# A graph layer with residual and layer norm: put and code turns in the unused columns of the pick banks, ranking products at the end of the step before, bias rows behind the table's stores

## The chip, the cores and the metric

One core of a Trainium2 chip runs the kernel. The metric is the device time of one execution in microseconds (us); lower is better. Engines are named as the profile names them: PE is TensorE (PEld its weight loads), DVE is VectorE, ACT is ScalarE, POOL is GpSimd, SP is SyncE, which here only issues DMAs. "L614" is line 614 of the kernel before.

## The reference

The graph has 12,500 nodes with 128 features and 400,000 edges that are sorted by their destination. Each edge has a type, 0 or 1. What is computed, cut to what matters:

```python
Xs = x[src]
m_data = Xs @ W_data.T + b_data
m_ctrl = Xs @ W_control.T + b_control
msg = where(edge_type == 0, m_data, m_ctrl)
agg = segment_sum(msg, dst, num_segments=12500)
h = x + relu(agg + (x @ W_self.T + b_self))
out = (h - mean(h)) / sqrt(var(h) + 1e-5)
```

## The kernel before, in words

**The idea.** Weights are linear, so the kernel first adds up the source rows of each destination node, apart for the two edge types, and counts them; the product with W_data and W_control, the counts times the biases, the self term and the norm come once for each node ("finish"). A float32 row is held as three bf16 parts (384 columns), so that bf16 matmuls add it up without loss.

**Tiling.** The 3125 blocks of 128 edges fall into 25 groups of 125 blocks, and each group into windows of two kinds. "p" windows (5 blocks, 865 blocks in all) gather their source rows from a table in DRAM, rows3, by an indirect DMA on POOL for each block (`msg`, L721), and are added up by a selection matrix `psel` (L671, L747). "e" windows (20 blocks, 113 windows) take their source rows from a copy of the table in SBUF, x3, with matmuls. The main loop has one step for each e window, 113 steps; the p blocks are spread through it.

**An e window w** goes through these stages; each names its function:

- `give_slots(w)` sorts the window's 2560 edges into 100 cells (node blocks) of 32 places each. `block_matrix`, `fours` and `same_lane` (DVE) write a one-hot matrix O and sums of it (`prod`). `before` (PE, L550) multiplies these with triangular matrices, the *ranking products*, into the bank `rk`; L492 adds a column for the spares of the window before it. `ranks` (DVE, L560 to L575) turns them into each edge's place within its cell, and `rank_matrix` into `rv` (L602). `over` (DVE) picks out the few edges that have no place in their cell and counts them (`over_n`).
- `put` (PE, L614, 20 full-width matmuls of 64 columns) writes node numbers and codes into their cells, in columns 0 to 63 of `rk`. `spread` copies them to SBUF (`cell`, ACT, L622), and two DMAs on SP send the node numbers through DRAM to all partitions (`there`, `pick`).
- `turn_codes` (PE, L634, four 128x32 matmuls of 25 columns, into columns 100 to 124 of `rk`) and `keep_codes` (ACT, L644) turn the codes. With them run the third and fourth part of `spare_slots` for window w-1: seven matmuls (L502) with the 128x64 matrices `om`, three ACT and DVE copies, and so the row numbers `idx` of the spares.
- `pick_matrix(w)` (DVE, L656) makes `pick` one-hot.
- `picked(w)` is the step itself, in six *units* t = 0 to 5. Each unit does two pairs of `rows(q)`: eight `pick` matmuls of 128x32 (L769) write two banks of a `got` tile, 384 of the 512 columns in each, and ACT copies both into `emsg` (L780). There are two `got` tiles, used in turn. A unit also does `count(q)` for four q of the unit before it (L798, 128x32) and `add` (L671, twelve full-width matmuls of 176 columns). Unit 2 gathers the spares' rows (`spare_rows`, POOL, L784, into `last`), unit 5 does `last_rows` (two more picks and an ACT copy, L793). `choose` (DVE, L476) makes the selection matrices `esel` for eight or nine q. `end` adds the last q and accumulates the window's sums into `acc` (DVE, L709); it is called as `ending` in unit 0 of the next step.

**The order of the work.** Each step hands lists of (position, function) to `merged`, which calls them by position; unit t stands at (t + 0.5) / 6. In step w, before the change: the ranking products of window w+2 in unit 1, `ranks` at 0.26, `rank_matrix` at 0.3, the spares' `om` at 0.28, `over` at 0.75; O, `fours` and `same_lane` of window w+3 at 0.55; `pick_matrix(w+1)` at 0.6; `put` and `spread` of window w+2 at the end of unit 4; its `turn_codes` and `keep_codes` in `end`. From the calls, the framework builds one queue for each engine, which it may order otherwise where operands are ready at other times; on the chip each queue is worked off in order. `rk` is one bank; the products of window w+3 can only be written when every reader of window w+2's is done.

**Start-up.** `split_x` loads x, splits it into x3 (L254 to L257) and stores it as the table rows3 with eight SP DMAs (L261). Meanwhile `all_slots` puts windows 0 and 1 into their cells. Then come, in the order of the calls: the loads of group 1 (L193 to L201, 21 DMAs), `bparts`, which splits the biases on one partition (DVE) and writes them into nine places of `bias` by 27 SP DMAs (L405, L407), `pick_matrix(0)`, the first slots of window 2, `store_rows`, and 14 `fetch` calls (POOL gathers of p blocks). `bias` is first read by the finishing products (L894).

Of the kernel before, what the change touches and what calls it, by code (L numbers as in the profile page):

```python
# [151 lines left out]
def short_path(ctx, tc, const, ident, eps, wT, brow, bad, x, src, dst, etype, ws, bs, out):  # L152
# [172 lines left out]

    ltri = keep.tile([P, 4, P], BF, name="ltri")
# [67 lines left out]

    def bparts():

        part = tmp.tile([1, 3, 3, D], BF, name="part")
        rest = tmp.tile([1, 3, D], FP, name="rest")
        nc.vector.tensor_copy(part[:, 0], brow)
        nc.vector.tensor_tensor(rest, brow, part[:, 0], op=OP.subtract)  # L400
        nc.vector.tensor_copy(part[:, 1], rest)
        nc.vector.tensor_tensor(part[:, 2], rest, part[:, 1], op=OP.subtract)
        for at in [at + k for at in range(0, P, CAP) for k in (0, 3)]:
            for j in range(3):
                nc.sync.dma_start(out=bias[at + j:at + j + 1, :, :], in_=part[:, j, 0:2, :])  # L405
        for j in range(3):
            nc.sync.dma_start(out=bias[6 + j:7 + j, 0, :], in_=part[:, j, 2, :])  # L407
# [76 lines left out]
    def spare_slots(w, rk):  # L484


        if w < 0:
            return [lambda: None] * 4
        s = slots[w]

        def over_before():
# [4 lines left out]
        def over_matrix():  # L496
            om = s["om"] = two.tile([P, TOP, OVF], BF, name="om", bufs=1)
            nc.vector.tensor_scalar(om, slot_col, rk[:, 500:501], None, op0=OP.is_equal)

        def turn():  # L500
            for k in range(TOP):
                nc.tensor.matmul(  # L502
                    rk[:OVF, 504:507], s["om"][:, k, :], s["bits"][:, :, k],
# [3 lines left out]
        def keep():  # L507
            code = s["code"][:OVF, NQ - 1:NQ]
            nc.scalar.copy(code, rk[:OVF, 506:507].rearrange("p (n o) -> p n o", o=1).to_broadcast(list(code.shape)))
            part = two.tile([OVF, 2], FP, name="part")  # L510
            nc.scalar.copy(part, rk[:OVF, 504:506])
# [6 lines left out]
    def give_slots(w):  # L518
# [26 lines left out]
        def before():  # L545
# [8 lines left out]
            spares = s["spares"] = spare_slots(w - 1, rk)  # L554
            spares[0]()
# [53 lines left out]
        def put():  # L609


            for c in range(EC):
                m = P if c < EC - 1 else NCELL
                nc.tensor.matmul(  # L614
                    s["rk"][:m, :2 * CAP], s["held"][:, c * NCELL:c * NCELL + m], s["rv"][:, c].rearrange("p v r -> p (v r)"),
# [15 lines left out]
        def turn_codes():  # L631

            for a in range(4):
                nc.tensor.matmul(  # L634
                    s["rk"][CAP * a:CAP * (a + 1), 100:100 + NQ], s["cell"][:, CAP:], ident_b[:, a * NQ:(a + 1) * NQ],
                    start=True, stop=True, skip_group_check=True,
                )
            s["spares"][2]()

        def keep_codes():  # L640
            rk = s["rk"]
            code = s["code"] = two.tile([P, NQ, 2], BF, name="code")
            at = rk[:, 100:100 + NQ].rearrange("p (n o) -> p n o", o=1)
            nc.scalar.copy(code, at.to_broadcast(list(code.shape)))  # L644
            s["spares"][3]()
# [107 lines left out]
    def picked(w, tiled, ending, fin_used, before):  # L753
# [20 lines left out]
        def rows(q):  # L774
            ps = psg.tile([P, pair, 512], FP, name="got")
            msg = two.tile([P, pair, 3 * D], BF, name="emsg", bufs=5)
            for k in range(pair):
                pick(ps[:, k, :3 * D], q + k)
                s["msg"][q + k] = msg[:, k, :]
            nc.scalar.copy(msg, ps[:, :, :3 * D])  # L780

        def spare_rows():
            msg = s["msg"][NQ - 1] = two.tile([P, 3 * D], BF, name="last")
            nc.gpsimd.indirect_dma_start(  # L784
                out=msg[:OVF, :], out_offset=None, in_=rows3[:, :],
                in_offset=bass.IndirectOffsetOnAxis(ap=slots[w]["idx"], axis=0),
            )
# [19 lines left out]
        def unit(t):  # L807

            for q in range(t * per, (t + 1) * per, pair):
                rows(q)  # L810
            if t == 1 and before:
                before()
# [367 lines left out]
```

## Time and profile before

| what | value |
|---|---|
| median of three runs | 2107.02 us (2105.46 to 2108.23) |
| the profiled execution | 2095.26 us, of which the span is 2093.6 us |
| busy in the span: PE, DVE, ACT, POOL | 1836.4, 1720.3, 1304.5, 1305.9 us |
| TensorE clock granted, mean | 0.978 |
| picks L769 | 10896 matmuls, 663.5 us busy |
| sums L671 of esel | 8136 matmuls, 761.9 us busy |
| copy emsg L780 | 1356, 803 ns each |
| gathers msg L721 | 865, 1350 ns each |

Busy is the time in which at least one instruction of the engine runs. Matmuls overlap, so the length of one matmul says little, and the distance from start to start is what a stream of them costs. A wait is the idle time of an engine just before an instruction, put down to what came last of all that the instruction needed. The profile is of one execution, and its own time (2095.26 us) is the one to compare its parts with.

### The profile page before, as it was taken

What the parts mean: (1) busy time and instruction counts of PE and PEld (TensorE: products, weight loads), DVE (VectorE), ACT (ScalarE), POOL (GpSimd) and SP (SyncE); (2) the same over time, 40 slices, a digit from 0 to 9 for tenths busy, and PEclk for the clock granted to TensorE, in tenths of its full rate; (3) what the DMA queues carried; (4) which work ended last, traced back from release to release, by engine and by line L of the source; (5) the groups of instructions that cost most, each with busy time, mean ns of one, the idle gap of its engine ahead of it and who ended that gap; (6) DMA issues with size and microseconds to landing.
All of it is one profiled execution on the core that took longest, in us unless ns stands there. A gap on an engine that the chain in (4) does not pass through costs nothing.

```text
span 2093.6 us, 75473 instructions
## 1 busy us (share of the span) xinstructions
PE 1836.4 (88%) x30869; PEld 1376.5 (66%) x30869; DVE 1720.3 (82%) x4707; ACT 1304.5 (62%) x2464; POOL 1305.9 (62%) x996
## 2 busy tenths in 40 slices
PE   0669889999999998999999999999999999999996
PEld 0446667666766676666666666766776676766675
DVE  7958889888888888888888878878888888878873
ACT  4535666666666665666666666656666666656665
POOL 0167667667667566667666556575667667766760
PEclk9989999999999999999999999999999999999998
DMA  7643443443443443433433434434434434434321
GB/s 187 193 123 115 122 136 101 137 135 100 133 135 99 135 133 95 137 111 117 135 108 108 127 99 136 131 100 134 132 102 132 131 111 131 120 105 130 124 96 32
DMA packets 187343, 254.92 MB, mean 122 GB/s; under 512 B 86202, under 2 KB 153804, under 8 KB 183916
## 3 DMA queue, kind: packets, MB, share of 16 engines
q1 hardware_dynamic: 129226, 152.97, 22.7%
q0 software_dynamic: 45136, 90.65, 15.5%
q10 hardware_dynamic: 12626, 6.40, 1.2%
q8 instruction: 243, 3.98, 0.8%
q14 instruction: 112, 0.92, 0.1%
HBM read 231.87 MB, written 18.03 MB: 119 GB/s over the span
## 4 chain that ended last, share of the span: by engine, by line
PE 57%; DVE 28%; issue 5%; ACT 5%; DMA 2%; SPq 1%; POOL 1%; DVEq 0%; another core or an unknown queue 0%; ACTq 0%; POOLq 0%
PE sums L671 25%; PE got L769 19%; ACT emsg L780 4%; DVE esel L476 3%; PE rk L614 3%; DVE pick L656 3%; DVE prod L564 3%; DVE rv L602 2%; PE sums L798 2%; PE fin L894 2%; DVE found L573 2%; DVE prod L542 2%; PE rk L502 2%; DVE ahead L560 2%; PE rk L550 1%
## 5 line engine op out<-in xcount | busy, mean ns | idle before, releaser
L721 POOL DMA_INDIRECT msg<-rows,pidx x865 | 1167.3, 1350 | 697.9 <-PE sums L671 236.2
L780 ACT CAST emsg<-got 128x768 bf16<-128x768 f32 x1356 | 1036.1, 803 | 522.6 <-PE got L769 387.6
L671 PE MATMUL sums<-esel,emsg 128*128 128x176 bf16 x8136 | 761.9, 242 | 14.3 <-issue 13.4
L769 PE MATMUL got<-x,pick 128*32 128x384 bf16 x10896 | 663.5, 334 | 77.5 <-ACT emsg L780 43.8
L671 PEld LDWEIGHTS <-emsg 128*128 128x128 bf16 x8136 | 603.0, 99 | 174.6 <-issue 157.6
L769 PEld LDWEIGHTS <-pick 128*32 128x32 bf16 x11074 | 258.7, 95 | 232.6 <-issue 131.2
L476 DVE TENSOR_TENSOR esel<-code_col,code 128x1408 bf16<-128x1408 bf16 x339 | 308.6, 910 | 31.7 <-PE sums L671 14.1
L709 DVE TENSOR_TENSOR acc<-acc,sums 128x352 f32 (+2 forms) x238 | 102.0, 428 | 175.3 <-PE sums L671 85.8
L671 PE MATMUL sums<-psel,msg 128*128 128x48 bf16 x2595 | 187.3, 185 | 17.5 <-issue 7.2
L798 PE MATMUL sums<-esel,one_col 128*32 128x176 bf16 x2825 | 181.7, 244 | 7.0 <-issue 6.3
L784 POOL DMA_INDIRECT last<-rows,idx x113 | 134.4, 1189 | 56.4 <-issue 16.5
L671 PEld LDWEIGHTS <-msg 128*128 128x128 bf16 x2595 | 150.7, 98 | 26.0 <-issue 23.6
L614 PE MATMUL rk<-rv,O 128*128 128x64 bf16 x2260 | 90.8, 195 | 70.9 <-DVE rv L602 64.8
L656 DVE TENSOR_SCALAR pick<-pick,lane_f 128x1600 bf16<-128x1600 bf16 x226 | 143.2, 639 | 8.5 <-issue 5.0
L614 PEld LDWEIGHTS <-O 128*128 128x128 bf16 x2260 | 83.1, 100 | 99.2 <-issue 98.3
L747 PE MATMUL sums<-psel,one_col 128*128 128x48 bf16 x865 | 145.9, 183 | 0.5 <-issue 0.5
L476 DVE TENSOR_TENSOR O<-cell_col,blk 128x2000 bf16<-128x2000 bf16 x113 | 134.6, 1191 | 12.2 <-PE fin L769 4.7
L564 DVE TENSOR_TENSOR prod<-O,ahead 128x2000 bf16<-128x2000 bf16 x113 | 134.4, 1189 | 0.0
L560 DVE TENSOR_REDUCE ahead<-rk 128x100 bf16<-128x500 f32 x113 | 76.2, 674 | 53.5 <-PE got L769 21.0
L798 PEld LDWEIGHTS <-one_col 128*32 128x32 bf16 x2825 | 86.6, 96 | 47.5 <-issue 17.7
L747 PEld LDWEIGHTS <-one_col 128*128 128x128 bf16 x865 | 82.9, 96 | 1.0 <-issue 0.9
L573 DVE TENSOR_REDUCE found<-half 128x20 f32<-128x520 bf16 x113 | 77.1, 683 | 0.0
(173 smaller groups left out, 2030.2 us busy)
## 6 DMA issues: line engine op xcount, KB each, us to landing
pick<-there SPq DMA_DIRECT2D x113, 800.0 KB
acc<-acc_start SPq DMA_DIRECT2D x23, 1280.0 KB
msg<-rows,pidx POOLq DMA_INDIRECT x865
rows<-x SPq DMA_DIRECT2D x6, 1344.0 KB
xs<-in_x_dram SPq DMA_DIRECT2D x99, 62.5 KB
out_dram<-h SPq DMA_DIRECT2D x99, 62.5 KB
xt<-in_x_dram ACTq DMA_DIRECT2D x6, 896.0 KB
there<-cell SPq DMA_DIRECT2D x113, 6.2 KB
```

The source lines that it names most:

```text
L476: nc.vector.tensor_tensor(sel.rearrange("p n (w t) -> p n w t", t=2), col[:rows].rearrange("p (o w t) -> p o w t", o=1, t=2).to_broadcast( ...
L564: nc.vector.tensor_tensor(prod, s["O"], ahead.rearrange("p (o j) -> p o j", o=1).to_broadcast([P, EC, NCELL]), op=OP.mult)
L573: nc.vector.tensor_reduce(found, half[:, :, :26], AX.X, OP.add)
L614: nc.tensor.matmul(s["rk"][:m, :2 * CAP], s["held"][:, c * NCELL:c * NCELL + m], s["rv"][:, c].rearrange("p v r -> p (v r)"), start=(c == ...
L656: nc.vector.tensor_scalar(t, t, lane_f, None, op0=OP.is_equal)
L671: nc.tensor.matmul(out, msg[:, j * D:(j + 1) * D], sel, start=(start and j == 0), stop=stop, skip_group_check=True)
L721: nc.gpsimd.indirect_dma_start(out=msg[:, k, :], out_offset=None, in_=rows3[:, :], in_offset=bass.IndirectOffsetOnAxis(ap=codes["p", g][0] ...
L747: nc.tensor.matmul(cnt, one_col, sel, start=False, stop=(c == n - 1), skip_group_check=True)
L769: nc.tensor.matmul(ps[CAP * a:CAP * (a + 1), :], slots[w]["pick"][:, a * NQ + q, :], x3[:, 4 * q + a - a0].rearrange("p j d -> p (j d)"), ...
L780: nc.scalar.copy(msg, ps[:, :, :3 * D])
L784: nc.gpsimd.indirect_dma_start(out=msg[:OVF, :], out_offset=None, in_=rows3[:, :], in_offset=bass.IndirectOffsetOnAxis(ap=slots[w]["idx"], ...
L798: nc.tensor.matmul(cells_of(s["ps"], EW, 1)[CAP * (q % 4):CAP * (q % 4 + 1), :], one_col[:, :CAP], s["sel"][q], start=(q < 4), stop=(q + 4 ...
```

## The change

Put writes columns 384 to 511 of the second `got` bank of unit 5's second pair, and the code turns and the spares' products those of unit 0's second pair in the step after. In unit 5 the counts, the last picks (unless finishing work is in the step) and put come between the pair's picks and its ACT copy. `rk` then serves the ranking products alone; those of window w+3 are issued at the end of unit 5 of step w. `ranks` goes to position 0.02, `rank_matrix` to 0.1, `om` to 0.2. `om` becomes a kept tile with one more block of zeros, and its seven products take 128 columns of weights (two neighbouring blocks), so that they have the full width. In the start-up, the split biases go to DRAM with one DMA; after the table's stores come the spares' gather for step 0, nine DMAs for the bias rows, and the loads of group 1.

The diff, cut to its core:

```diff
+    om_all = keep.tile([P, TOP + 1, OVF], BF, name="om_all")
+    nc.vector.memset(om_all, 0.0)
...
+    b_parts = dram.tile([3, 3, D], BF, name="b_parts")
     def bparts():
...
+        nc.sync.dma_start(
+            out=b_parts.rearrange("j i d -> (j i d)").rearrange("(o e) -> o e", o=1),
+            in_=part.rearrange("o j i d -> o (j i d)"),
+        )
+
+    def bias_rows():
         for at in [at + k for at in range(0, P, CAP) for k in (0, 3)]:
-            for j in range(3):
-                nc.sync.dma_start(out=bias[at + j:at + j + 1, :, :], in_=part[:, j, 0:2, :])
-        for j in range(3):
-            nc.sync.dma_start(out=bias[6 + j:7 + j, 0, :], in_=part[:, j, 2, :])
+            nc.sync.dma_start(out=bias[at:at + 3, :, :], in_=b_parts[:, 0:2, :])
+        nc.sync.dma_start(out=bias[6:9, 0, :], in_=b_parts[:, 2, :])
...
-        def over_matrix():
-            om = s["om"] = two.tile([P, TOP, OVF], BF, name="om", bufs=1)
-            nc.vector.tensor_scalar(om, slot_col, rk[:, 500:501], None, op0=OP.is_equal)
+        def over_matrix(rk):
+            nc.vector.tensor_scalar(om_all[:, :TOP], slot_col, rk[:, 500:501], None, op0=OP.is_equal)
-        def turn():
+        def turn(at):
+            om = om_all.rearrange("p k o -> p (k o)")
             for k in range(TOP):
                 nc.tensor.matmul(
-                    rk[:OVF, 504:507], s["om"][:, k, :], s["bits"][:, :, k],
+                    at, om[:, k * OVF:k * OVF + P], s["bits"][:, :, k],
...
-        def put():
+        def put(at):
...
-                    s["rk"][:m, :2 * CAP], s["held"][:, c * NCELL:c * NCELL + m], ...
+                    at[:m, :2 * CAP], s["held"][:, c * NCELL:c * NCELL + m], ...
-        def spread():
+        def spread(at):
             cell = s["cell"] = two.tile([P, 2 * CAP], BF, name="cell")
-            nc.scalar.copy(cell, s["rk"][:, :2 * CAP])
+            nc.scalar.copy(cell, at[:, :2 * CAP])
...
-                    s["rk"][CAP * a:CAP * (a + 1), 100:100 + NQ], s["cell"][:, CAP:], ...
+                    at[CAP * a:CAP * (a + 1), :NQ], s["cell"][:, CAP:], ...
-            s["spares"][2]()
+            s["spares"][2](at[:, 32:35])
...
-        s["tiled"] = {4: [put, spread], 6: [turn_codes, keep_codes]}
+        s["put"], s["turn"] = (put, spread), (turn_codes, keep_codes)
...
-            (0.1, before), (0.26, ranks), (0.28, lambda: s["spares"][1]()), (0.3, rank_matrix), (0.75, over),
+            (0.02, ranks), (0.2, lambda: s["spares"][1](s["rk"])), (0.1, rank_matrix), (0.75, over),
...
-        def rows(q):
+        def rows(q, more=None):
...
+            if more:
+                more[0](ps[:, pair - 1, 3 * D:])
             nc.scalar.copy(msg, ps[:, :, :3 * D])
+            if more:
+                more[1](ps[:, pair - 1, 3 * D:])
...
+            def counts_and_put(at):
+                counts()
+                if not fin_used:
+                    last_rows()
+                put[0](at)
+
+            rows(t * per)
+            if t == 0 and turn:
+                rows(pair, turn)
+            elif t == turns - 1 and put:
+                rows(t * per + pair, (counts_and_put, put[1]))
+            else:
+                rows(t * per + pair)
...
-            if t == 1 and before:
-                before()
...
+            if t < turns - 1 or not put:
+                counts()
+            if t == turns - 1 and (fin_used or not put):
                 last_rows()
+            if t == turns - 1 and before:
+                before()
             if t > 0:
                 add((t - 1) * per, t * per)
-            for u in tiled.get(t, []):
-                u()
...
-    load(1, "e")
-    load(1, "p")
     bparts()
...
+    slots[2]["before"]()
     store_rows()
+    spare_rows(0)
+    bias_rows()
+    load(1, "e")
+    load(1, "p")
```

More of the change, by code (lines that the diff above doesn't have):

```diff
@@ L553, in before @@
                 )
-            spares = s["spares"] = spare_slots(w - 1, rk)
-            spares[0]()
+            s["spares"] = spare_slots(w - 1)
+            s["spares"][0](rk)
         def ranks():
@@ L751, in gathered, with spare_rows, picked @@
         return evenly([lambda c=c: chunk(c) for c in range(n)])
-    def picked(w, tiled, ending, fin_used, before):
+    def spare_rows(w):
+        msg = slots[w]["last"] = two.tile([P, 3 * D], BF, name="last")
+        nc.gpsimd.indirect_dma_start(
+            out=msg[:OVF, :], out_offset=None, in_=rows3[:, :],
+            in_offset=bass.IndirectOffsetOnAxis(ap=slots[w]["idx"], axis=0),
+        )
+    def picked(w, put, turn, ending, fin_used, before):
         g, i = each_e[w]
@@ L807, in unit, with counts @@
         def unit(t):
-            for q in range(t * per, (t + 1) * per, pair):
-                rows(q)
-            if t == 1 and before:
-                before()
+            def counts():
+                if t > 0:
+                    for q in range((t - 1) * per, t * per if t < turns - 1 else NQ):
+                        count(q)
+            def counts_and_put(at):
[10 more added lines that the diff above has]
+                rows(t * per + pair)
             if t in (0, 1):
@@ L979, in ending @@
         pass
+    turn = None
     for w in range(pairs):
```

72 lines of the change are left out of this document (34 added, 38 removed).

## The prediction

> **What bounds the kernel now.** I read the page first: the busy shares, then the chain of work that ended last.
>
> ```profile
> PE 1836.4 (88%) x30869; PEld 1376.5 (66%) x30869; DVE 1720.3 (82%) x4707; ACT 1304.5 (62%) x2464; POOL 1305.9 (62%) x996
> ...
> PE 57%; DVE 28%; issue 5%; ACT 5%; DMA 2%; SPq 1%; POOL 1%; DVEq 0%; another core or an unknown queue 0%; ACTq 0%; POOLq 0%
> ```
>
> PE is nearly full, but over a quarter of the chain runs through DVE, so DVE makes PE wait somewhere. The waits, longest first, say where:
>
> ```profile
> PE rk L614 <- DVE rv L602: 64.8, 43, 18.5
> ...
> PE got L769 <- ACT emsg L780: 43.8, 95, 1.5
> ...
> PE sums L671 <- DMA last<-rows,idx: 10.4, 1, 10.4
> ```
>
> The columns are total us, times, longest. The first is put waiting for the rank matrix; two of its 43 waits (18.47 and 12.12 us, before 70 us) are start-up, so 34.2 us in 41 waits lie in the loop. The third is one hole in the start-up.
>
> The stretch 130 to 2045 us holds PE 1756.28 and DVE 1611.21 us busy in 1915: PE is idle 159 us, the most that removing waits alone can bring there. The rest must come from PE's own work. Here is a step boundary in the timeline (start, length):
>
> ```profile
> 1009.79 0.40 PE L671 MATMUL sums<-esel,last 128*128 128x176 bf16 x3
> 1010.12 0.20 PE L634 MATMUL rk<-ident_b,cell 128*32 128x25 bf16 x4
> 1010.25 0.39 PE L502 MATMUL rk<-bits_b,om 128*64 128x3 bf16 x7
> 1010.57 0.25 PE L671 MATMUL sums<-psel,msg 128*128 128x48 bf16 x3
> ...
> 1010.87 0.83 PE L769 MATMUL got<-x,pick 128*32 128x384 bf16 x16
> 1011.64 0.41 PE L550 MATMUL rk<-prod,ltri 128*128 128x125 bf16 x4
> 1011.88 0.16 PE L492 MATMUL rk<-over_n,ltri 128*128 128x1 bf16 x1
> 1011.98 0.26 PE L798 MATMUL sums<-esel,one_col 128*32 128x176 bf16 x4
> ```
>
> Groups overlap, so a cost is the distance from a start to the next start. Sixteen picks followed by counts (also 128*32) take 0.66 us (median of 296 places); followed by L550 (128*128), 0.77 (78 places). Twelve sums followed by full-width work take 0.92, by picks 1.01. So each change between 128*32 and full width costs PE 0.09 to 0.11 us, inside its "busy" time.
>
> From the same timeline I cut the loop into 108 steps at L634: mean 17.62 us (DVE busy 14.83, ACT 11.26). The 84 without finishing products last 17.01 (DVE 14.09), the 24 with them 19.76 (DVE 17.42).
>
> **The change, part by part, on PE.**
>
> Ranking products (L550, L492): now between picks and counts, 98 times of 113. They cost 0.11 + 0.25 + 0.09 = 0.45 us. In the new place, full-width work follows them: 0.25 + 0.03 = 0.28. Gain 0.17 x 98 = 17 us.
>
> Code turns (L634, L502): now after full-width sums: 0.33 for three sums instead of 0.23 at full width's pace, so 0.10; then 0.13 and 0.32; 0.55 in all. In the new place the four 25-column turns follow picks; bounded by nothing and the 0.13 of their row, I take 0.05, nearest to what four counts stream in (0.08 by nine counts to 0.32). The seven spare products become full width: 0.027 each by the psel row (three to 0.08), 0.046 if nothing changes, so 0.19 to 0.32; I take 0.19. The change to full width was there anyway. Gain 0.31 x 113 = 35 us (ends 14 and 42).
>
> Put (L614): 59 of 113 stand between two pick groups, because rv came late: two changes, 0.19. In the new place put ends the tiled stretch. Gain 0.19 x 59 = 11 us.
>
> The wait for rv: ahead now starts 0.25 of a step in, and rv ended at 1021.76 for a put at 1022.26. New: the ranking products are done before the step begins. From ahead (1012.09) to rv's end is 9.7 us, so rv is there some 10 us into the step and put is wanted at about 15. All 34 us go.
>
> Steady sum: 17 + 35 + 11 + 34 = 97 us. DVE work is the same; one memset is added once. The zeroed eighth column block lies beside start-up work and costs nothing; on PE's path it would be under 0.5 us.
>
> What is late next: ACT. Put now writes the bank whose two picks the 0.80 us copy (L780) reads. Does that copy wait for put? Two rows of today say that readers wait for the bank's last writer, though they read other columns:
>
> ```profile
> DVE ahead L560 <- PE rk L492: 19.4, 34, 1.4
> ...
> ACT code L644 <- PE rk L502: 12.3, 31, 0.8
> ```
>
> So I assume it does. From the second pair's first pick: picks 0.33, counts 0.32, last picks 0.26, put 0.60 and its tail 0.16: put ends at 1.67. The copy of the last picks (0.47), put ahead of it on ACT, ends by about 1.5. Then 0.80 and the cell copy 0.21: the bank is free at 2.68. PE wants it at 1.51 + 0.28 (ranking products) + 0.92 (sums) + 0.11 (a chunk) + 0.44 (first pair) = 3.26. Slack 0.58 us. At the code turns the same sum gives 1.9 against 2.3: slack 0.4. Hidden, but thinly; without cover (ACT late by a whole copy, 0.8) it costs 0.2 + 0.4 = 0.6 a step. I charge 0.15 a step, a quarter of that: 16 us.
>
> [...] Were only columns to count, the copy would start 1.2 us earlier and the charge be nil.
>
> **Start-up.** SP's queue and POOL:
>
> ```profile
> 74.00 6.82 SPq L405 DMA_DIRECT2D bias<-part  x11
> 80.86 1.85 SPq L407 DMA_DIRECT2D bias<-part  x3
> 82.76 6.44 SPq L261 DMA_DIRECT2D rows<-x  x3
> ```
>
> The 27 bias issues fill 18.5 us of SP ahead of the last three table stores. Their data were ready at 65.75 (the last L257). POOL's gathers start at 95.14, once the table is there, 14 of them 1.26 us apart; only then comes `last` (115.72), for which PE stands idle 10.4 us until 118.34. After it PE idles 4.03 more until the accumulation has ended at 124.56. Now one bias issue stands ahead of the stores, so they start up to 16 us sooner; `last` for step 0 is POOL's first gather. Nine bias issues and 21 loads move behind the stores: by L405's 0.63 they take 5.7 us, and the loads today 14 (26.60 to 40.60). The loads were issued from 26.60 on, ahead of everything, in idle queue time; if they really go behind, the preparation of group 1 (DVE at 86.18) waits 0 to 5 us. The hole goes (10.4), the 4.03 perhaps: ends 5 and 15; I take 12.
>
> **Sum.** 97 - 16 + 12 = 93 us. The profiled execution took 2095.26 us (span 2093.6, 1.66 around it): 2002. The runs' median, 2107.02, is 11.8 above it (0.6%); a saving of work carries over, so 2107 - 93 = **2014 us**.
>
> **Rivals.**
>
> *DVE takes over* (chance 0.18). The ranking products now need over_n of the previous slot, which DVE makes last in its step: ahead, all of the step's DVE work, over_n, products, ahead again is a loop. For it: DVE is 84% busy. Against: from ahead to over_n it took 12.46 us here, plus products and hand-overs 0.7: 13.2 in a step of some 16; in finishing steps 17.42 + 0.7 = 18.1 against 19.2. If DVE keeps its waits of today except the one for rk (2.79 idle less 0.5), a step is 14.83 + 2.3 = 17.1: gain 0.5 x 108 + 12 = 66, **2041 us**.
>
> *The pick matrix comes late: slower* (0.10). Put moves from behind the fifth unit's sums to the sixth's last picks (1.3 us later than today's late put), and cell stands behind a 0.80 copy. `there` and `pick` follow, on SP, so pick lands about 2.1 us later; today DVE compares it (L656) 8.6 us after cell. DVE works in order, so if L656 keeps its place everything on DVE waits. PE itself wants pick only 16 us after cell. It decides once DVE's wait exceeds 0.5 us a step (17.62 - 17.1, above). At 1 us, half the delay: 18.1 a step, 54 - 12 = 42 us lost: **2149 us**. Against: only 3.0 us of such waits today, and L656's place follows the order that the schedule is built in.
>
> *It doesn't do what it says* (0.08). The traces show that issue order isn't program order (put of the fifth unit runs among the sixth's picks). If products and turns are again put between tiled groups, only the rv wait and start-up remain, less the ACT charge twice: 34 + 12 - 32 = 14: **2093 us**.
>
> *The forecast* (0.64): 1975 (all 97, 15 at the start, and half of the 43.8 us of PE waiting for ACT, since 30.8 us of ACT waiting for put go) to 2040 (ends of the code turns and of the start-up, full ACT charge).
>
> **Numbers.** The forecast and DVE's case hold 0.82; with their bounds the range is 1972 to 2062. About 0.2% (4 us) is what a measurement tells from no change: faster 0.87 (forecast, DVE, most of the third), same 0.03, slower 0.10.
>
> **What would show it.** L614's wait for rv gone from the loop; L550 followed by L671; L634 following L769; put's distance 0.60; PE's wait for emsg at or below 60 us; `last` first on POOL, no 10 us hole. Wrong if L656 waits for DMA in most steps, if L492 waits for over_n, or if PE's wait for emsg exceeds 100 us.

## The result: slower by 4.1%

The changed kernel took 2193.48 us (median of 4 runs, 2187.24 to 2198.97), the kernel before 2106.42 us beside it (4 runs, 2105.46 to 2108.23): ratio 1.0411, interval 1.038 to 1.0442. The forecast was 2014 us. The profiled execution took 2191.1 us with a span of 2189.0 (before: 2095.26 and 2093.6), at a mean granted clock of 0.958 (before 0.978).

Busy times and the chain of waits after the change, from the page:

```profile
PE 1830.7 (84%) x30869; PEld 1394.9 (64%) x30869; DVE 1742.3 (80%) x4708; ACT 1295.9 (59%) x2464; POOL 1292.5 (59%) x996
...
PE 55%; DVE 21%; issue 10%; ACT 6%; DMA 3%; another core or an unknown queue 1%; DVEq 1%; POOL 1%; SPq 0%; ACTq 0%; POOLq 0%
```

PE is as busy as before, over a span 95 us longer. DVE's share of the chain went down, as meant; "issue", time in which an engine waits for nothing that the profile shows, doubled from 5% to 10%. PE's waits (total us, times, longest):

```profile
PE sums L677 <- issue: 46.1, 105, 1.8
PE got L782 <- ACT emsg L795: 42.0, 91, 2.1
PE got L621 <- issue: 32.9, 62, 1.2
PE rk L621 <- DVE rv L611: 31.1, 2, 19.0
...
PE got L782 <- ACT part L520: 17.2, 23, 1.7
```

Put's wait for the rank matrix (L621 is the old L614) is left in its two start-up places only. Between 130 us and the last step, waits put down to "issue" are 286 with 128.2 us, against 141 with 54.5 before. I call them stalls.

The stalls have a companion. TensorE's granted clock stood at half in 34 stretches of 3.4 to 6.8 us in the loop, 147 us in all; before, in 13 stretches, 55 us. In 26 of the 34, PE had stalled for 1 us or more in the 6.8 us ahead of the stretch (0.43 us in the mean of all such windows). A probe below (m2) shows what half a clock costs: the same 14 products took 1.22 us at a granted clock of 1.00 and 2.26 us at 0.50. So the 92 us more at half clock cost at most some 46 us, an estimate from these figures, and the profile counts that time as busy.

A step boundary without a stall reads as the prediction wanted it:

```profile
1008.18 0.78 PE L621 MATMUL got<-rv,O 128*128 128x64 bf16 x20
1008.79 0.40 PE L559 MATMUL rk<-prod,ltri 128*128 128x125 bf16 x4
...
1009.05 1.07 PE L677 MATMUL sums<-esel,emsg 128*128 128x176 bf16 x12
...
1011.04 0.20 PE L641 MATMUL got<-ident_b,cell 128*32 128x25 bf16 x4
1011.17 0.34 PE L511 MATMUL got<-bits_b,om_all 128*128 128x3 bf16 x7
1011.37 1.07 PE L677 MATMUL sums<-esel,emsg 128*128 128x176 bf16 x12
```

Ranking products (L559) stand between put and sums, code turns (L641) behind picks, put takes 0.61 us. In 28 of 105 steps put takes over 1 us, as here:

```profile
344.49 0.35 PE L621 MATMUL got<-rv,O 128*128 128x64 bf16 x6
345.07 0.25 PE L621 MATMUL got<-rv,O 128*128 128x64 bf16 x3 [0.23 <-issue]
345.80 0.26 PE L621 MATMUL got<-rv,O 128*128 128x64 bf16 x3 [0.48 <-issue]
346.54 0.23 PE L621 MATMUL got<-rv,O 128*128 128x64 bf16 x2 [0.48 <-issue]
```

This put takes 4.4 us, two or three products in each 0.74 us, though all its inputs are there. In the same microseconds POOL issues message gathers back to back: 343.00, 344.25, 345.51, 346.81, with 0.30 us between them. In 72 of the 105 steps PE stalls for over 0.5 us. Cut by POOL's timeline, PE stood still for 41% of the time in which POOL issued the sixth or a later gather of such a run (107 us of it; before: 18% of 68 us), and 2 to 3% beside the first two.

Over 108 steps cut at the code turns, a step now takes 18.49 us (before 17.62). Changes between 128*32 and full width fell from 18.5 to 13.3 a step; PE's idle time rose from 1.39 to 2.33 us.

Start-up: POOL's queue and PE's first long stall.

```profile
75.80 1.08 POOL L761 DMA_INDIRECT last<-rows,idx  x1 [71.00 <-DMA bias<-b_parts]
77.18 1.17 POOL L727 DMA_INDIRECT msg<-rows,pidx  x1 [0.30 <-issue]
```

```profile
87.03 0.83 PE L782 MATMUL got<-x,pick 128*32 128x384 bf16 x8 [4.29 <-issue]
```

Gathers start 19 us sooner, `last` first, and the 10.40 us hole is gone. But 19 gathers in one run (75.80 to 100.2) now lie beside PE's first two steps, and the six longest of PE's stalls there are 4.29, 1.10, 1.42, 1.53, 1.80 and 1.09 us, 11.2 in all. The fifth set of code turns (the third behind the start-up's two) comes at 143.2 us, against 141.7 before.

### The profile page after: what moved, and what is told of

The parts are those of the page before. It is cut to its first block, busy times and chain, and to the rows that moved or that the text cites. A ratio compares the mean times of both kernels' runs of the same rounds, so it can differ in the third digit from the quotient of the medians.

```text
span 2189.0 us, 75225 instructions
## 1 busy us (share of the span) xinstructions
PE 1830.7 (84%) x30869; PEld 1394.9 (64%) x30869; DVE 1742.3 (80%) x4708; ACT 1295.9 (59%) x2464; POOL 1292.5 (59%) x996
## 4 chain that ended last, share of the span: by engine, by line
PE 55%; DVE 21%; issue 10%; ACT 6%; DMA 3%; another core or an unknown queue 1%; DVEq 1%; POOL 1%; SPq 0%; ACTq 0%; POOLq 0%
PE sums L677 24%; PE got L782 19%; ACT emsg L795 4%; PE got L621 4%; PE sums L808 3%; DVE prod L573 2%; DVE esel L485 2%; DVE O L485 2%; PE fin L917 2%; DVE acc L715 2%; DVE pick L662 1%; PE rk L559 1%; DVE ahead L569 1%; DVE rv L611 1%
## 5 line engine op out<-in xcount | busy, mean ns | idle before, releaser
L727 POOL DMA_INDIRECT msg<-rows,pidx x865 | 1117.9, 1292 | 713.1 <-PE sums L677 353.6
L795 ACT CAST emsg<-got 128x768 bf16<-128x768 f32 x1356 | 1049.1, 802 | 646.7 <-PE got L782 346.3
L677 PE MATMUL sums<-esel,emsg 128*128 128x176 bf16 x8136 | 785.5, 245 | 42.6 <-issue 38.4
L782 PE MATMUL got<-x,pick 128*32 128x384 bf16 x10896 | 655.5, 338 | 108.5 <-ACT emsg L795 42.0
L677 PEld LDWEIGHTS <-emsg 128*128 128x128 bf16 x8136 | 618.1, 100 | 157.5 <-issue 144.1
L761 POOL DMA_INDIRECT last<-rows,idx x113 | 170.5, 1509 | 151.3 <-DMA bias<-b_parts 71.0
L808 PE MATMUL sums<-esel,one_col 128*32 128x176 bf16 x2825 | 172.9, 242 | 36.9 <-DVE acc L715 19.3
L677 PEld LDWEIGHTS <-msg 128*128 128x128 bf16 x2595 | 160.1, 98 | 41.0 <-issue 36.9
L662 DVE TENSOR_SCALAR pick<-pick,lane_f 128x1600 bf16<-128x1600 bf16 x226 | 138.8, 652 | 7.0 <-DMA pick<-there 7.0
L621 PEld LDWEIGHTS <-O 128*128 128x128 bf16 x2260 | 83.3, 101 | 93.2 <-issue 88.3
L621 PE MATMUL got<-rv,O 128*128 128x64 bf16 x2220 | 99.8, 196 | 33.3 <-issue 32.9
L803 ACT CAST last<-fin 64x384 bf16<-64x384 f32 x89 | 42.1, 473 | 62.2 <-PE rk L501 42.6
```

Of the source, the lines that this page charges most:

```text
L621: nc.tensor.matmul(at[:m, :2 * CAP], s["held"][:, c * NCELL:c * NCELL + m], s["rv"][:, c].rearrange("p v r -> p (v r)"), start=(c == 0), s ...
L662: nc.vector.tensor_scalar(t, t, lane_f, None, op0=OP.is_equal)
L677: nc.tensor.matmul(out, msg[:, j * D:(j + 1) * D], sel, start=(start and j == 0), stop=stop, skip_group_check=True)
L727: nc.gpsimd.indirect_dma_start(out=msg[:, k, :], out_offset=None, in_=rows3[:, :], in_offset=bass.IndirectOffsetOnAxis(ap=codes["p", g][0] ...
L761: nc.gpsimd.indirect_dma_start(out=msg[:OVF, :], out_offset=None, in_=rows3[:, :], in_offset=bass.IndirectOffsetOnAxis(ap=slots[w]["idx"], ...
L782: nc.tensor.matmul(ps[CAP * a:CAP * (a + 1), :], slots[w]["pick"][:, a * NQ + q, :], x3[:, 4 * q + a - a0].rearrange("p j d -> p (j d)"), ...
```

## The experiments

**Theory A**: a run of back-to-back indirect gathers on POOL slows PE's issue, and the change made runs fall where they hurt. **Rival B**: the new order and the shared banks cost the time; stalls only come with it. Variants came up on the way. H1: DVE stands still for put, and POOL's catching up then falls beside PE's work. H2: POOL stands for idx ahead of `last` and issues a run behind it. C: gathers slow what PE is fed with, and it costs most where short products stand together at the step's end. D in v1 and v2: only the rate of the gathers beside a shorter step counts; D in p1: codes and idx come later. Each group ran beside the kernel before, whose medians lay between 2087 and 2108 us from group to group, so ratios are compared.

### Start-up alone, loop alone

```diff
 (e1_start: into the kernel before; e2_loop: taken out of the changed one)
-    load(1, "e"); load(1, "p")
     bparts()          # with b_parts, one issue
...
     store_rows()
+    spare_rows(0)
+    bias_rows()
+    load(1, "e"); load(1, "p")
```

> The kernel before with only the start-up part of the change: one bias issue ahead of the table's stores, the others, the loads of group 1 and the first `last` gather behind them. Where it stands now: in the changed kernel the marks of steps 3 and 4 lay at 126.4 and 143.2 us against 120.0 and 141.7 before, so the start-up seems to have won nothing although POOL began 19 us sooner. Theory A (a run of back-to-back indirect gathers on POOL slows PE's issue, and the run now falls on PE's first steps): same as before within 0.5%, 2097 to 2112 us. Rival B (the gathers do PE nothing; the start-up's gain of about 12 us was only lost to the changed loop): 2090 to 2097 us.

> The changed kernel with the start-up of before: only the loop's part of the change. Both theories put the loss in the loop. A: 2180 to 2200 us, as the changed kernel. B: start-up gain missing as well, 2195 to 2210 us.

Measured: start-up alone 2105.07 us, ratio 1.0004 (0.9975 to 1.0032); loop alone 2192.88 us, 1.0431 (1.0387 to 1.0476). The start-up's part is worth nothing, the loss is all in the loop. Both fit A; B's start-up gain isn't there.

### Without message gathers, and with plain transfers

```diff
 (e3_before_few, e4_after_few)
+            if len(kept) == HOLD:
+                kept.append(kept.pop(0)); fetched.append(kept[-1])
+                return
 (e5_after_plain)
-                nc.gpsimd.indirect_dma_start(out=msg[:, k, :], ...)
+                nc.gpsimd.dma_start(out=msg[:, k, :], in_=rows3[P * (at % 90):P * (at % 90) + P, :])
 (e10_after_half)
+            if n_all[0] > HOLD and n_all[0] % 2:
+                fetched.append(fetched_last[0])
+                return
```

> The kernel before with the message gathers left out after the first 18: the loop's message products read the first 18 tiles in turn, so the output's message part is left out; products, waits for `last` and everything else stay. Theory A: the 141 issue stalls (54.5 us) in PE's loop go, and with them late signals; the wait for the rank matrix stays: 2030 to 2060 us. Rival B (stalls are a thing of PE's dense short work, or of the order): no more than the gathers' own waits go, 2085 to 2105 us.

> The changed kernel with the message gathers left out after the first 18, as in the run beside it. Theory A: the 288 issue stalls (129 us) go and the clock comes back, and what the prediction counted is seen at last: 1980 to 2030 us, below the kernel before without gathers by 20 to 70 us. Rival B (the order costs it: put stands between the picks and ScalarE's copy, O waits for put): 2140 to 2190 us, still 50 us or more above the kernel before without gathers.

> The changed kernel with a plain transfer of 128 rows in place of each indirect message gather, on the same queue, with the same bytes; which rows of the table are read is the part of the computation that changes. Theory A, if it is the indirect gathers on POOL that do it: 1885 to 1930 us, near the 1885 of the changed kernel without gathers. If it is the bytes and the writes into the tiles: 2100 us or more. Rival B: 2140 to 2190 us.

> The changed kernel with every second message gather left out after the first 18 (two chunks use one tile, so half of the messages are wrong rows). 308 us lie between all and none. Theory C with an edge in the rate: nearly all of it goes, 1885 to 1930 us. If every gather costs a fixed time: half of it, 2020 to 2060 us.

| message gathers | kernel before | changed kernel |
|---|---|---|
| all | 1 | 1.0411 (1.038 to 1.0442) |
| every second | not run | 1951.9 us, 0.9317 (0.9252 to 0.9382) |
| none after 18 | 1926.84 us, 0.9156 (0.9123 to 0.9188) | 1884.98 us, 0.8954 (0.8922 to 0.8985) |
| plain transfers | not run | 1882.86 us, 0.8928 (0.8874 to 0.8982) |

This is the main result. Without gathers the changed kernel is the faster one, by 42 us, with the same order on PE as with them. All message gathers together cost the kernel before 8.4% of its time, 181 us, and the changed one 308 us (14.6% of the time of before), far more than I expected of either. Stalls in the loop fall from 54.5 and 128.2 us to 0.0 and 0.2, and time at half clock from 55 and 147 us to 4 and 14. Plain transfers of the same bytes into the same tiles on the same queue cost nothing (1882.86 us against 1884.98 without gathers), so bytes and writes aren't it. (They keep POOL busy for 705 us in all instead of 1293; that a busy POOL alone does no harm is shown by the additions of m2, below: 250 products in 19.13 us beside them, in 21.53 with nothing beside.) Half the gathers give back three quarters of the loss (0.109 of 0.146): more than by number, less than an edge would give. B falls. The pages without gathers, before and changed:

```profile
PE 1747.5 (91%) x30869; PEld 1349.8 (70%) x30869; DVE 1705.4 (89%) x4707; ACT 1300.7 (68%) x2464; POOL 140.0 (7%) x149
...
DVE 53%; PE 33%; DMA 6%; issue 3%; ACT 2%; another core or an unknown queue 1%; DVEq 1%; SPq 1%; ACTq 0%
```

```profile
PE 1695.0 (90%) x30869; PEld 1343.8 (71%) x30869; DVE 1708.7 (91%) x4708; ACT 1283.5 (68%) x2464; POOL 231.6 (12%) x149
...
DVE 59%; PE 23%; issue 5%; DMA 4%; ACT 4%; DVEq 3%; another core or an unknown queue 1%; SPq 0%; ACTq 0%
```

The change takes 52.5 us of PE's own time away. What is left is bounded by DVE, 91% busy and 59% of the chain: PE's waits for `acc` are 45.5 us here and were 5.2 in the kernel before without gathers. So even without gathers the change is worth 42 us and not the 93 of the forecast.

### What a gather does to the other engines

```python
# m1, m2: mm() is one product; gathers and products of a phase are called together
for k in range(24): gather(kind)      # indirect 128 rows / 64 rows / 256 B; or plain
for k in range(count): mm(ps, n)      # n = 176, 48 or 384 columns
# m3: ScalarE releases each gather
nc.scalar.copy(long_out[:, :size], long_in[:, :size])
nc.scalar.copy(at, long_out[:, 0:1])  # the gather's index
```

> None of the reference's work: a stream of products on PE alone (500 of 128x176, then 900 of 128x48, then 240 of 128x384), each width four times: with nothing beside it, with 24 indirect gathers of 128 rows of 768 B back to back on POOL, with the same 24 and a POOL instruction between each two, and with 24 plain transfers of the same size on POOL's queue. Theory A (back-to-back gathers slow PE's issue): in the second phase of each width stretches in which a product takes 0.2 us or more instead of some 0.08, from the third to sixth gather on; in the third few or none; in the fourth none. If the limit is in the instructions PE is fed with, the 48-wide phase loses most and the 384-wide least. Rival B: the four phases of a width are equal.

> None of the reference's work: streams of products on PE (128x176 unless said), each beside one load on POOL that starts with it: nothing; 24 gathers of 128 rows of 768 B back to back; the same of 64 rows; the same of 128 rows of 256 B; 24 plain transfers; 60 POOL additions; gathers one by one, each released by PE after 8, 14, 20 or 26 products; groups of 4 and of 8 released after 20 products for each; then a stream of small copies on DVE, and one on ACT, beside 24 gathers; then PE with 48 and with 384 columns beside 24 gathers. Theory A with a rate: an undisturbed stream takes 0.08 us a product; beside 24 gathers it falls to one in 0.7 us or more after some six gathers (6 us); plain transfers and POOL's additions leave it alone; gathers one in 20 or 26 products (1.6 and 2.1 us apart) leave it alone or nearly, one in 8 doesn't; groups of 8 disturb it and groups of 4 don't. If rows or bytes make the load, 64 rows or 256 B halve it. If the disturbance is in how all engines are fed, DVE's and ACT's copies slow down as well; if it is in PE alone, they keep their 0.1 us or so. Rival B: nothing but the 24 gathers one behind the other shows any effect, at any rate of PE's.

> None of the reference's work: a stream of products on PE beside 24 indirect gathers that ScalarE releases at an even pace, by copies of 3000, 2500, 2100, 1800, 1500, 1200 and 900 columns (some 3.3 down to 1.3 us apart, by an estimate of 1.04 us for 1000 columns from the 0.80 us of the 768-column copy); 176-column products, then 48 and 384 columns beside the 2100 and the 1500 pace. Theory C (an indirect gather slows the supply of instructions; PE holds some 60 to 90 products in store): no stall at 3.3 and 2.8 us, as in the paced phases of the run before; stalls from some pace between 2.6 and 1.5 us on, sooner for 48 columns than for 384. If every gather takes a fixed amount of supply, the products done per us fall in proportion to the gathers per us, with no edge.

In m1 the gathers of the later widths were issued during the 176-column phases, so it says nothing of width. It does show that POOL instructions between gathers (0.43 us each, gathers 1.55 us apart) don't bring PE back to full pace: behind 40 gathers without a gap one product in 2.8 us, behind 25 up to four in 1.4 us. From m2's timeline: undisturbed; beside 24 gathers from 27.22 on (last at 56.38); with 48 and with 384 columns; and DVE's copies beside 24 gathers:

```profile
4.96 21.53 PE L108 MATMUL ps<-mov,mat 128*128 128x176 bf16 x250 [4.96 <-DVE mat L105]
27.16 6.62 PE L108 MATMUL ps<-mov,mat 128*128 128x176 bf16 x85 [0.66 <-DVE mat L105]
34.28 0.48 PE L108 MATMUL ps<-mov,mat 128*128 128x176 bf16 x4 [0.51 <-issue]
...
56.93 0.30 PE L108 MATMUL ps<-mov,mat 128*128 128x176 bf16 x1 [1.78 <-issue]
...
61.16 11.36 PE L108 MATMUL ps<-mov,mat 128*128 128x176 bf16 x126 [0.26 <-issue]
...
892.64 2.58 PE L108 MATMUL ps<-mov,mat 128*128 128x48 bf16 x60 [0.66 <-DVE mat L105]
...
938.89 15.20 PE L108 MATMUL ps<-mov,mat 128*128 128x384 bf16 x91 [0.70 <-DVE mat L105]
```

```profile
745.87 20.19 DVE L143 COPY dvt<-mat 128x64 bf16<-128x64 bf16 x80
...
769.15 0.18 DVE L143 COPY dvt<-mat 128x64 bf16<-128x64 bf16 x1 [1.08 <-DVE dvt L143]
```

PE runs 60, 85 and 91 products freely, in 2.58, 6.62 and 15.20 us. What passes before the first stall is nearer to a number of products than to a time. From there on products trickle, down to one in 0.7 to 2.8 us, and full pace is back 4.8 us after the last gather has begun. DVE slows as well, after 80 copies and 21 us, and ScalarE after 72 copies and 20 us. So in m2 a run of 24 indirect gathers slowed the pace at which all three engines start instructions, after these delays. That their supply of instructions runs dry (theory C) is argued, not shown. Gathers of 64 rows, and of 256 B, slow PE as well: from 72.5 to 155.72 us, beside them, it did some 611 products in 83 us, where the undisturbed pace gives 53 (an estimate from the rows above and the plain transfers below); 60 POOL additions do nothing (250 products in 19.13 us). The 24 plain transfers were issued ahead of their own phase, from 151.81 to 164.67 us; beside them PE came back to full pace at 155.72 and did 139 products in 12.82 us. Gathers that PE released one by one stood some 3.2 us apart or more, whether behind 8 or 26 products, and all left PE alone, so the paces of 1.6 and 2.1 us that were expected weren't reached here. Groups of four gathers with a pause leave PE alone; groups of eight cost five stalls each, 0.26 to 0.97 us long.

In m3, 176 columns ran without any stall at every pace, down to gathers some 1.6 us apart (0.7 us of it POOL waiting); only 48 columns were disturbed, 0.2 us in every 73 products at 2.19 us, once for each gather, and up to 0.42 at 1.69. For 176 columns stalls came with gathers 1.27 us apart that waited for nothing (m2), and none with gathers 1.6 us apart that did (m3); where between them they begin, no run shows.

### Space between gathers in the kernels

```diff
 (e6: behind each message gather, in the changed kernel and in the one before)
+                for _ in range(3): nc.gpsimd.iota(dull, pattern=[[0, 16]], base=0, channel_multiplier=0)
```

> The changed kernel with three small POOL instructions (0.13 us each in the start-up of before) behind each message gather, so that gathers stand some 0.7 us apart instead of 0.3; PE's order is the same. Theory A, if the run of gathers matters: stalls fall from 129 us to below 60, 2090 to 2160 us. If only the number of gathers counts: within 1% of 2193. Rival B: no gain, or a loss by POOL's longer queue, 2190 to 2220 us.

> The kernel before with the same three POOL instructions behind each message gather. Theory A: its 54 us of stalls fall to some 25, 2060 to 2100 us. If only the number of gathers counts: 2100 to 2115 us. Rival B: 2107 to 2130 us.

Measured: 2557.76 us, 1.2114 (1.2035 to 1.2194), and 2499.28 us, 1.1836 (1.1757 to 1.1914). Much slower, against every expectation. But these runs say nothing of space between gathers. The instructions wait for nothing, and the framework put most of them ahead of the gathers in POOL's queue (the first row is of the tile they write, with the ns of one and the times of the first and the last; the second is a wait of PE):

```profile
L730 POOL IOTA dull<- x2595: 131/141/1280, 4.8 to 849.3; 128x16 int32 x200
...
PE sums L677 <- DMA last<-rows,idx: 392.2, 22, 27.4
```

All 2595 were done by 849 us, when 164 of the 865 gathers had been issued, and in 744 of the 864 places between two gathers there is none. Up to then POOL is late with `last`: PE waits 392 us for it, 387 in the kernel before, which is about the whole loss (364 us against the changed kernel, 392 against the one before). Behind 849 us a step takes 18.50 and 17.88 us, much as without these instructions (18.49 and 17.62). The stalls are 113 and 66 us. Whether space between gathers helps a kernel was not tested.

### Which part makes the runs worse

```diff
 (e7_O_later)
+            with tc.issue_after(slots[w - 1]["ranked"].ins) if w > 2 else ExitStack():
                 select(s["O"], cell_col, blk2)
 (e8_last_later)            if t == 2:  ->  if t == 4:      (gather of last)
 (e9_ahead17)               AHEAD = 14  ->  AHEAD = 17
 (v1_put_sooner)            elif t == turns - 1 and put:  ->  elif t == turns - 2 and put:
 (v2_rank_old)              if t == turns - 1 and before:  ->  if t == 1 and before:   (and ranks, om, rank_matrix at their old positions)
 (p1_turns_only)            rows(t * per + pair, turn if t == 0 else None)   in the kernel before, with the full width
 (p2_wide_only)             rk[:, 504:507], om[:, k * OVF:k * OVF + P]       in the kernel before
```

> The changed kernel with O's select held behind the slot's ranks on DVE, so that DVE no longer stands still at the step's end for put (162 us of waits, 12 before) while POOL gathers. Theory H1 (this standstill gathers POOL's catching-up into runs beside PE): stalls fall by half or more, 2060 to 2140 us. Theory H2 (POOL stands longer for idx ahead of `last`, and the run follows that): 2180 to 2200 us. Rival B (put ahead of the copy costs it): 2180 to 2200 us. Scheduling on PE changes with it, so within 15 us nothing follows.

> The changed kernel with the gather of `last` issued two units later in POOL's queue; PE's order is the same. POOL stood 32 us for idx ahead of `last`, 11 before. H2: 2120 to 2170 us, fewer runs of eight and more. H1: within 1% of 2193. Rival B: the same.

> The changed kernel with the message gathers issued 17 instead of 14 chunks ahead, with the same 18 buffers: POOL's next gather is then always tied to a buffer that PE has just freed, and `last` stands three gathers later in its queue; PE's order is the same. H2 (POOL gets ahead, stands at `last`, then runs): 2100 to 2170 us. H1: 2180 to 2205 us. Rival B: 2193 within 1%.

> The changed kernel with put one unit sooner (in the second pair's bank of the fifth unit instead of the sixth), so that its 20 short products no longer stand between the last counts and the ranking products. Everything else of the change stays. Theory C: the stalls of the last third of the step (107 of 129 us) fall by half or more, 2080 to 2150 us. Rival B (put ahead of ScalarE's copy costs it): nothing won, 2180 to 2200 us. Rival D (only the gathers' rate beside a shorter step counts, not where the short products stand): 2170 to 2200 us. A wait for the rank matrix may come back, up to 35 us.

> The changed kernel with the ranking products where they were before (after the second unit's picks of the next step), put and code turns as changed. Theory C: five short products fewer in the stretch, a part of the loss goes, 2140 to 2185 us, less is won than with put moved. Rival D: 2170 to 2200 us. If the wait for the rank matrix comes back whole, 34 us of it are added.

> The kernel before with the code turns alone changed: next to the second picks of the following step, in their bank, the spare products at full width. Ranking products, put and start-up stay as before. The prediction's terms for this part: 35 us gained, less about half of the 16 us charged for ScalarE waiting in the shared bank, so ratio 0.985 to 0.99. Rival D (codes and idx come later, ScalarE and POOL's `last` wait for them, and PE's picks wait for ScalarE's part and cell copies, 29 us in the changed kernel): 1.00 to 1.015. If put's move is what costs the remaining 28 us, this run is at or below 1.0; if the turns cost them, it is near 1.014.

> The kernel before with the spare products (seven of 3 columns a step) at 128 instead of 64 rows out, and nothing else: the same order on PE, the same banks. One of three width changes around the code turns goes, 0.09 to 0.11 us by the prediction's rows, and 0.13 us if each of the seven runs at full width's pace: 10 to 25 us, ratio 0.988 to 0.996. If time saved on PE is eaten by starvation between gathers (theory C: PE faster, gathers closer together): 0.997 to 1.003.

| kernel | us | ratio to before | stalls in the loop, us |
|---|---|---|---|
| changed | 2193.48 | 1.0411 (1.038 to 1.0442) | 128.2 |
| e7, O behind the ranks | 2238.27 | 1.0666 (1.0591 to 1.0742) | 150.0 |
| e8, `last` later | 2181.32 | 1.0414 (1.035 to 1.0479) | 127.3 |
| e9, 17 ahead | 2172.33 | 1.0376 (1.0318 to 1.0434) | 124.8 |
| v1, put one unit sooner | 2209.84 | 1.0559 (1.0472 to 1.0646) | 118.4 |
| v2, ranking products where they were | 2124.99 | 1.0141 (1.007 to 1.0213) | 65.7 |
| p1, code turns (and full width) alone | 2127.55 | 1.0162 (1.0131 to 1.0192) | 57.7 |
| p2, full width alone | 2086.54 | 0.996 (0.9935 to 0.9985) | 60.3 |

H1 and H2 are not borne out: e7 is slower, though it also changed PE's order, and e8 and e9 stay within the interval of the changed kernel. That put's short products at the step's end are the price, the second half of C, falls with v1: 20 products fewer there, and nothing won. v2 won more than any theory allowed (2125 us against 2140 to 2200). Two parts carry the loss. The ranking products' move is 2.7% (v2 against the change, some 57 us of 2107) and half of the stalls. The code turns' move with its full width is 1.6% (p1, some 34 us), without more stalls to speak of; put's move adds nothing that the intervals tell (p1 against v2). p2 is the only part that wins, 0.4% or some 8 us, and the only version that beats the kernel before with all its gathers.

What p1 loses stands in its waits:

```profile
DVE idx L516 <- ACT part L514: 155.2, 77, 7.2
POOL last L789 <- DVE idx L516: 90.7, 51, 10.2
PE rk L617 <- DVE rv L605: 75.4, 53, 18.5
...
PE got L770 <- ACT part L514: 23.7, 42, 1.5
```

Before, these were 14.3, 11.4, 64.8 and none. The code turns come a pick group later, so idx comes later too, and DVE stands ahead of it; ScalarE's part copy keeps the shared bank, and PE's next picks wait for it. With 9 us more of waiting for emsg (52.8, 43.8 before), PE waits some 43 us more.

Why the ranking products' place doubles the stalls I can show only in part. In the changed kernel 2.45 of DVE's 3.36 idle us a step lie in the eighth to eleventh twelfth of the step, and 0.96 of the 1.19 us of stalls. In v2 DVE's idle time lies around the step's start, where PE does 384-column picks, and stalls are spread thinly, 0.61 us. Without gathers those twelfths hold 0.71 us of DVE's idle time (e4), so most of it goes when the gathers go. My reading: put ends late, DVE waits for it, POOL's gathers run on, and one feeds the other. That order of cause is argued, not shown.

## Why the prediction was wrong, step by step

- **The bound** ("PE is idle 159 us, the most that removing waits alone can bring there"): wrong as a bound on what PE loses to others. 54.5 of them were stalls put down to "issue", in the trace of before for anyone to add up, and behind them stood a cost of 181 us (e3) in the kernel before, much of it inside PE's "busy" time (1836.4 against 1747.5 without gathers). I took the gathers for hidden work.
- **PE's terms** (17 + 35 + 11 = 63 us for fewer width changes): mostly borne out without gathers, where PE's busy time falls by 52.5 (1747.5 to 1695.0). With gathers it falls by 5.7 only (1836.4 to 1830.7); products at half clock (up to 46 us more, the estimate above) and products that trickle count as busy. The full width for the spare products, 0.13 us a step or 15 of the 35, gave some 8 us alone (p2). The ranking products were worth 17 in the sum; their move to the step's end cost some 57 us (v2).
- **The wait for rv** (34 us): gone from the loop, as said. In its place the loop has 74 us more of stalls; that one became the other isn't shown.
- **"What is late next: ACT"**, 16 us: mis-sized and incomplete. PE's wait for emsg stayed (42.0), but waits for part (17.2) and cell (12.3) add 28 us, where 1.1 us for part stood before. That the copy waits for the bank's last writer was right: `ACT emsg L795 <- PE got L511` has 33.1 us in 66 waits. The step followed the copies and stopped; idx behind them, with DVE's order and POOL's queue waiting on it, was not followed. Code turns: a gain of 35 forecast, a loss of some 34 measured.
- **DVE takes over**: the rival was right about the limiter once gathers are gone (e4), though not about its gain: 42 us, where it summed 66. With the gathers it is not what made the kernel slower; DVE's share of the chain fell from 28% to 21%.
- **Start-up** (12 us): every sign came (stores sooner, `last` first, no hole), and the gain was nothing (e1). A run of 19 gathers moved onto PE's first steps, and the six longest stalls beside it make 11.2 us, about what had been won.
- **The bounds**: from its own figures the code turns' term runs from 11 to 41 us, not from 14 to 42, and the full charge for ACT, 0.6 us in 108 steps, is 65 us, where the upper end of 2040 holds 16. Neither brings 2193 us into the range.
- **"A saving of work carries over"**: this is the step that failed. Here gathers on POOL, 1% of the chain, slowed PE, 55% of it (181 us in the kernel before, 308 in the changed one). A stall's price was put at nothing, though 141 stalls stood in the trace. All the signs named under "What would show it" came, and none of the three named for "wrong if": L662 waits 7.0 us for its transfer in all, L501 not for over_n, and PE's wait for emsg is 42 us. The rivals looked for one new wait. What the loop lost, 0.87 us in each of 108 steps or 94 us, is by an estimate from the rows above: stalls 74, half clock up to 46, ACT's copies 28, PE's waits for `acc` 22 (29.3, 7.2 before), less 34 for rv and 52 of PE's work.

## What to carry to other kernels

Add up PE's "issue" waits before anything else: here they came in a regular beat beside runs of indirect gathers (two or three products in each 0.74 us) and went with them (128.2 us in the loop to 0.2), and a plan that moves runs of gathers beside other work of PE may be paid there. Look at the granted clock behind the stalls as well (147 us at half in the changed kernel's loop). The cheapest test is the kernel without its gathers, or with plain transfers in their place; it tells in one run what they cost and what a change would be worth without them. And look at the timeline of a probe before reading its time: in e6 the instructions stood elsewhere than they had been written. When a step moves, follow each small result to the engines that stand for it (in p1 DVE 155.2 us ahead of idx, then POOL 90.7 us ahead of `last`), not only to the bank it is read from.

## What the runs showed of the hardware

- Beside a run of 24 indirect gathers, PE's products began to stall after 60 of 48 columns, 85 of 176 and 91 of 384, DVE's copies after 80 and ScalarE's after 72 (m2). Gathers of 64 rows or of 256 B slowed PE too (some 611 products in 83 us instead of 53, an estimate). Plain transfers on POOL's queue (e5: 1882.86 us, 1884.98 without gathers; m2: 139 products in 12.82 us) and POOL's arithmetic (m2: 250 products in 19.13 us) didn't do it.
- In m1, 48-column products without gathers pause after 128 of them or a multiple, 0.37 us in seven places of nine and 0.62 and 0.64 in two; what makes them pause is not shown. The page lists transfers of instructions as a kind of their own (243 packets of 16 KB on q8 in the kernel before). That a late one stalls PE beside gathers, the trace speaks against: in m2 one such packet lies between 27 and 61 us, at 37.4 us. PE did 124 products in that time, and it went on trickling until 61 us, long behind the packet. What in a gather slows the engines, no run here shows. Every run's span and clock are on record, so all were recorded while they ran, and whether the recording takes part is open too.
- Stalls go with stretches of half clock: 147 us of the loop in the changed kernel, 55 before, 4 and 14 without message gathers; 14 products took 2.26 us at 0.50 and 1.22 us at 1.00 (m2).
- In the start-up of the kernel before, a `msg` gather of 128 rows took POOL 0.95 us (114.46 us) and a `last` gather of 64 rows 0.91 (115.72 us): half the rows saved 0.04.
- Gathers that wait for another engine, some 1.6 us apart, leave 176-column products undisturbed (m3); with POOL working between them, 1.55 us apart and behind a run without gaps, PE kept trickling (m1). A kernel paced by waiting was not tried.
